# Group norm and attention on one core: constant products ahead of the input, a matrix product for the first group sums, eight open chains

## The chip, the cores and the metric

The kernel runs on one core of one Trainium2 chip. The metric is the device time of one execution in microseconds; a run's figure is that of its slowest core, and here there is only one core. The time before is the median of three runs.

## What is computed

The input x has 4 images of 512 channels and 48 x 48 pixels (2304 tokens). Each image goes through a group norm with 32 groups of 16 channels, a projection to q, k and v, attention with 8 heads of 64 channels, an output projection, and a residual sum. Cut to what matters:

```python
hn  = group_norm(x, gn_scale, gn_bias)              # 32 groups, eps 1e-5
qkv = einsum('oc,bchw->bohw', qkv_w, hn) + qkv_b    # float32
q, k, v = qkv.reshape(b, 3, 8, 64, t).astype(float16)
w = softmax(einsum('bhct,bhcs->bhts', q * s, k * s))
a = einsum('bhts,bhcs->bhct', w, v).astype(float32)
return x + einsum('oc,bchw->bohw', proj_w, a) + proj_b
```

A group's mean and variance need 16 channels, which are 16 partitions of the tile that holds x, so the sums have to cross partitions.

## The kernel before

Channels lie on partitions: an image is four chunks of 128 channels (index c), each in five token blocks (index j), four of 512 tokens and one of 256. Heads are treated in pairs, since two heads of 64 channels fill 128 partitions.

After an opening, a long stream runs over 16 groups (an image and a pair of heads), token blocks and bursts of key tiles. Each burst has scores on TensorE (L959), exponentials on ScalarE (L966), sums on VectorE (L1015) and the product with v on TensorE (L984). The projections of later groups (L709 for q and k, L760 for v, L848 for the output) are cut into pieces and put between the bursts. The order of every engine's instructions is the order in which the program issues them; each engine works in that order and waits on semaphores.

The change lies in the opening, which is what runs before the first scores. There the first image is loaded and normalised, and q and k of its first pair and v of its first two pairs are computed. What is needed to follow it:

- The loads. SP's queue brings the blocks of x chunk by chunk; two blocks of the first chunk and the first pair's weights go over ScalarE's queue; the four small vectors (scale, bias and so on) over GpSimd's. The remaining weights follow the last chunk of x on SP's queue.
- The small constants. GpSimd fills `mhalf`, `ones`, `ones16`, `fine`, `moments` and `nothing` (L571 to L923) after issuing its four loads.
- The statistics of a chunk. `stats` (L608) runs one VectorE pass over each block and `aggregate` (L612) joins the five into a mean and a variance per channel, in the columns of `moments`.
- From channels to groups. `group_scale` transposes `moments` on VectorE (L622), aggregates each half of 16 channels (L627), adds the epsilon (L629), raises to the power of minus one half on GpSimd (L631), and spreads the means back over the channels (L634). `coefficients` spreads the scales (L641), transposes back (L645) and forms a factor and an offset per channel (L651 to L653).
- The normalisation. `norm_chunk` applies them on ScalarE, block by block (L667), in place.
- The first chains. A chain is the sum over the four chunks for one block of q or k; `qk_steps` issues two products for a chunk, one for each half of 64 output columns (L709), and hands back the evacuation (L719, VectorE). Six chains stay open: the five blocks of k and the first of q. They take the six PSUM banks of the pool `ps_s`. When a chunk is normalised, its products go to all six. After the last chunk the six are evacuated, two at a time, and the other four blocks of q follow as closed chains (`qk_chain`), then the nine steps of v (`v_chain`).

VectorE's order in the opening is fixed by one loop: the statistics of the next chunk are placed between the coefficients of this one, with one block ahead of them for the first two chunks and two for the third.

PSUM has eight banks here: six in `ps_s`, one in `ps_av` (the products with v and the sums), one in `ps_w` (the projections in the stream and small products).

Of the kernel before, what the change touches and what calls it, by code (L numbers as in the profile page):

```python
# [12 lines left out]
F32 = mybir.dt.float32  # L13
F32R = mybir.dt.float32r
F16 = mybir.dt.float16
I32 = mybir.dt.int32
AF = mybir.ActivationFunctionType
ALU = mybir.AluOpType
# [6 lines left out]
GROUP = C // 32  # L25
EPS = 1e-5
P = 128
# [15 lines left out]
QB = 512  # L43
QBLOCKS = [(o, min(QB, T - o)) for o in range(0, T, QB)]
NQ = len(QBLOCKS)
# [422 lines left out]
def fast_path(  # L468
# [12 lines left out]
    nc = tc.nc  # L481

    RES = NC
    const = ctx.enter_context(tc.tile_pool(name="const", bufs=1))
# [4 lines left out]
    ppool = ctx.enter_context(tc.tile_pool(name="ppool", bufs=3))  # L489
# [3 lines left out]
    ps_s = ctx.enter_context(tc.tile_pool(name="ps_s", bufs=3, space=PSUM))  # L493
    ps_av = ctx.enter_context(tc.tile_pool(name="ps_av", bufs=1, space=PSUM))
# [24 lines left out]
    gsc = const.tile([P, NC], F32, name="gsc")  # L519
    gbi = const.tile([P, NC], F32, name="gbi")  # L520
# [49 lines left out]
    mhalf = const.tile([P, 2], F32, name="mhalf")  # L570
# [3 lines left out]
    ones16 = const.tile([P, D], F16, name="ones16")  # L574
    nc.gpsimd.memset(ones16, 1.0)

    fine = const.tile([P, 2 * QB // P], F32, name="fine")
    nc.gpsimd.memset(fine, 1.0)

# [4 lines left out]
    def chain_bank(name):  # L584
        if alone[0]:
            return ps_s.tile([P, 2, QB], F32, tag="ps", name=name)[:, 0, :]
        return ps_w.tile([P, QB], F32, tag="pw", name=name)

    def small_bank(name):
        return ps_w.tile([P, QB], F32, tag="pw", name=name)  # L590


    stat, coef, ab = {}, {}, {}
# [7 lines left out]
    moments = const.tile([P, 3, SQ], F32, name="moments")  # L601
    nc.gpsimd.memset(moments, 1.0)

    def stats(b, j, c):

        if b not in stat:
            stat[b] = small.tile([P, NC, NQ, 6], F32, tag="st", bufs=1, name=f"st_{b}")
        nc.vector.bn_stats(stat[b][:, c, j, :], hn[b, c, j])  # L608

    def aggregate(b, chunks=ALL):  # L610
        for c in chunks:
            nc.vector.bn_aggr(  # L612
                moments[:, 1:, c], stat[b][:, c].rearrange("p j s -> p (j s)")
            )

    def small_tile(n, tag):
        return small.tile([P, n], F32, tag=tag, bufs=1, name=tag)

    def group_scale(b, chunks=ALL):

        turned = small_tile(SQ * 3, "turned")
        nc.vector.transpose(  # L622
            turned.rearrange("p (c s) -> p s c", s=3), moments
        )
        grouped = small_tile(NGROUP * 2, "grouped").rearrange("p (g s) -> p g s", s=2)
        for i in range(NGROUP):
            nc.vector.bn_aggr(grouped[:, i, :], turned[:, bass.ts(i, GROUP * 3)])  # L627
        veps = small_tile(NGROUP, "veps")
        nc.vector.tensor_scalar(veps, grouped[:, :, 1], EPS, None, ALU.add)  # L629
        rstd = small_tile(NGROUP, "rstd")  # L630
        nc.gpsimd.tensor_tensor(rstd, veps, mhalf, ALU.pow)  # L631
        both = small_tile(SQ * 2, "both").rearrange("p (s c) -> p s c", s=2)
        spread = both.rearrange("p s (g j) -> p s g j", g=NGROUP)
        nc.vector.tensor_copy(  # L634
            spread[:, 0], grouped[:, :, 0:1].to_broadcast((P, NGROUP, GROUP))
        )
        coef[b, chunks[0]] = both, spread, rstd

    def coefficients(b, chunks=ALL):
        both, spread, rstd = coef.pop((b, chunks[0]))  # L640
        nc.vector.tensor_copy(  # L641
            spread[:, 1], rstd.unsqueeze(2).to_broadcast((P, NGROUP, GROUP))
        )
        cols = small_tile(SQ * 2, "cols").rearrange("p (s c) -> p s c", s=2)
        nc.vector.transpose(cols, both)  # L645
        cs = slice(chunks[0], chunks[-1] + 1)
        ga, mga, gb = (
            small.tile([P, NC], F32, tag=f"{n}{chunks[0] % 2}", name=f"{n}_{b}")[:, cs]
            for n in ("ga", "mga", "gb")
        )  # L650
        nc.vector.tensor_tensor(ga, cols[:, 1, cs], gsc[:, cs], ALU.mult)  # L651
        nc.vector.tensor_tensor(mga, cols[:, 0, cs], ga, ALU.mult)
        nc.vector.tensor_tensor(gb, gbi[:, cs], mga, ALU.subtract)  # L653
        for i, c in enumerate(chunks):
            ab[b, c] = ga[:, i : i + 1], gb[:, i : i + 1]

    def norm(b, j, c):
        t = hn[b, c, j]
        ga, gb = ab[b, c]
        nc.vector.tensor_scalar(t, t, ga, gb, ALU.mult, ALU.add)  # L660

    def norm_chunk(b, c):

        ga, gb = ab[b, c]
        for j in range(NQ):
            t = hn[b, c, j]
            nc.scalar.activation(t, t, AF.Identity, bias=gb, scale=ga)  # L667
# [27 lines left out]
    def qk_steps(g, part, j, bank=None):  # L695
        b, pr = divmod(g, NPAIR)
        o, n = QBLOCKS[j]
        pw = {0: bank}

        def one(c):  # L700
            if g not in qk:
                qk[g] = [
                    qkp.tile([P, T], F16, tag=a, name=f"{a}_{g}") for a in ("q", "k")
                ]
            if c == 0 and bank is None:
                pw[0] = chain_bank(f"pqk_{g}_{part}_{j}")
            w0 = part * C + pr * P
            for lo in (0, D):
                nc.tensor.matmul(  # L709
                    pw[0][lo : lo + D, :n],  # L710
                    wqkv[:, c, w0 + lo : w0 + lo + D],
                    hn[b, c, j],
                    start=(c == 0),
                    stop=(c == NC - 1),
                )

            def evacuate():
                col = part * NPAIR + pr
                nc.vector.tensor_scalar(  # L719
                    qk[g][part][:, o : o + n],  # L720
                    pw[0][:, :n],
                    bqkv[:, col : col + 1],
                    SCALE,
                    ALU.add,
                    ALU.mult,
                )

            if bank is not None:
                return evacuate
            if c == NC - 1:  # L730
                evacuate()

        return one

    def qk_chain(g, part, j):
        n = QBLOCKS[j][1]
        steps = qk_steps(g, part, j)
        return chain_pieces(n / 600.0, steps, HALVES if n == QB else WHOLE)
# [198 lines left out]
    av, acc, pts, avx, sums, rowd, ibs = {}, {}, {}, {}, {}, {}, {}  # L937

    stream = []
    for g in range(NG):  # L940
        for j, (o, n) in enumerate(QBLOCKS):
            count = NT * n // QB // BURST
# [255 lines left out]
    for b in range(B):  # L1198
        g = b * NPAIR
# [69 lines left out]

    six = [(1, j) for j in range(NQ)] + [(0, 0)]
    banks = [
        ps_s.tile([P, 2, QB], F32, tag="ps", name=f"ps_{i}") for i in range(3)
    ]
    chains = [qk_steps(0, *a, banks[i // 2][:, i % 2, :]) for i, a in enumerate(six)]

    def all_stats(c):
        for j in range(NQ):
            stats(0, j, c)  # L1280
        aggregate(0, (c,))

    all_stats(0)
    group_scale(0, (0,))
    for c in range(NC):

        for j in range(NQ):
            if j == (1 if c < 2 else 2):
                coefficients(0, (c,))
                norm_chunk(0, c)  # L1290
            if c + 1 < NC:
                stats(0, j, c + 1)
        if c + 1 < NC:
            aggregate(0, (c + 1,))
            group_scale(0, (c + 1,))
        for i, chain in enumerate(chains):
            evacuate = chain(c)
            if c == NC - 1 and i % 2 == 1:

                before()  # L1300
                evacuate()
            before = evacuate
    for j in range(1, NQ):
        for p in qk_chain(0, 0, j):
            p[1]()
    for i in range(0, NT, 2):
# [64 lines left out]
    for n in range(end):  # L1371
# [29 lines left out]
        if n - BEHIND in soon:  # L1401
            g, j = stream[n - BEHIND][:2]
# [9 lines left out]
    g, b, j = NG - 1, B - 1, NQ - 1  # L1412
    n = QBLOCKS[j][1]
# [6 lines left out]
    def last_banks(name):  # L1420
        return ps_s.tile([P, 2, QB], F32, tag="ps", name=name)
# [15 lines left out]
    def beyond(k, name, tag):  # L1437
        bank = chain_bank(name)
        _, store = last_run(k, bank)
        t = xpool.tile([P, QB], F32, tag=tag, name=f"beyond_{name}")  # L1440
        xt = res[b, k[0], k[1][0]].rearrange("p m n -> p (m n)")

        def copy():
            nc.scalar.copy(t, bank)

        def finish():
            nc.gpsimd.tensor_tensor(xt, t, xt, ALU.add)
            return store

        return copy, finish  # L1450
# [8 lines left out]
    copy, finish = beyond(ahead[0], "ahead_0", "x0_3")  # L1459
# [4 lines left out]
    for i, k in enumerate(todo[:NC]):  # L1464
        if i % 2 == 0:
            banks = last_banks(f"rest_{i}")
# [89 lines left out]
```

## Time and profile before

| | us |
|---|---|
| median of 3 runs | 1604.98 |
| lowest, highest | 1604.17, 1605.35 |
| profiled execution, its own time | 1605.03 |
| its span, first to last instruction | 1603.3 |
| TensorE busy (matmul) | 1577.8 (98%) |
| ScalarE busy | 1268.0 (79%) |
| VectorE busy | 1138.1 (71%) |
| GpSimd busy | 325.6 (20%) |

The opening by stretches, in the same profiled execution (us from the span's start; busy time of TensorE, VectorE, ScalarE and GpSimd):

| stretch | PE | DVE | ACT | POOL |
|---|---|---|---|---|
| 0 to 11.92, before the first product | 0 | 6.66 | 2.15 | 3.67 |
| 11.92 to 22.92, chunks 0 and 1 | 11.00 | 10.25 | 6.44 | 1.38 |
| 22.92 to 33.03, chunks 2 and 3 | 9.71 | 5.85 | 6.36 | 0.69 |
| 33.03 to 45.06, four more blocks of q | 12.03 | 3.65 | 0 | 0 |
| 45.06 to 76.24, v | 31.18 | 6.02 | 0 | 0 |

How to read it: the profile is one execution. PE is TensorE's matmul, PEld its weight load, DVE is VectorE, ACT ScalarE, POOL GpSimd, SP the engine that issues most loads and stores. In a line of the timeline the first number is the start, the second the time taken, then come the engine, the line of the kernel, the operation, what it writes and reads, and in brackets the idle time before it and what ended that. In a line of waits the three numbers are the total, the count and the longest. A float32 product appears as two matmuls and two weight loads.

### The profile page before, as it was taken

How to read it: one execution, taken by the hardware profiler on the slowest of the kernel's cores; microseconds unless marked ns; L12 is line 12 of the kernel's file. 1: busy time of each engine (PE TensorE's matmuls, PEld its weight loads, DVE VectorE, ACT ScalarE, POOL GpSimd, SP SyncE). 2: the span in 40 equal slices, each digit the busy share in tenths (PEclk: the TensorE clock that was granted, in tenths of full speed). 3: DMA queues.
4: the chain of work that ended last, by engine and by line, in shares of the span. 5: the costliest groups of instructions: out<-in, count | busy, mean ns of one | idle time of the engine just before them, and what ended most of it. 6: DMA issues, size and time to landing. Idle time of an engine off the chain costs nothing.

```text
span 1603.3 us, 28319 instructions
## 1 busy us (share of the span) xinstructions
PE 1577.8 (98%) x11500; PEld 692.1 (43%) x11500; DVE 1138.1 (71%) x1301; ACT 1268.0 (79%) x1362; POOL 325.6 (20%) x457
## 2 busy tenths in 40 slices
PE   6999999999999999999999999999999999999997
PEld 2533434443333534545333354455533334435544
DVE  6267668876666668887676666898766766667775
ACT  3077777888888888888888888887878888888895
POOL 1001202221121222322112121221212121122222
PEclk9999999999999999999999999999999999999998
DMA  7002021000000024521000001352100000015424
GB/s 216 9 14 64 14 59 29 18 15 11 14 15 12 15 64 120 147 67 28 11 14 18 14 12 41 112 156 87 25 15 18 15 15 11 15 31 177 137 67 128
DMA packets 94896, 82.10 MB, mean 51 GB/s; under 512 B 50852, under 2 KB 60964, under 8 KB 94756
## 3 DMA queue, kind: packets, MB, share of 16 engines
q1 hardware_dynamic: 92724, 78.35, 18.1%
q8 instruction: 92, 1.51, 0.4%
q10 hardware_dynamic: 1904, 1.84, 0.4%
q14 instruction: 48, 0.39, 0.1%
q0 software_dynamic: 128, 0.01, 0.0%
HBM read 60.70 MB, written 19.17 MB: 50 GB/s over the span
## 4 chain that ended last, share of the span: by engine, by line
PE 94%; DVE 3%; ACT 1%; DMA 1%; issue 0%; POOL 0%; SPq 0%; DVEq 0%
PE pqk L709 29%; PE ps L959 19%; PE av L984 19%; PE pv L760 15%; PE pr L848 8%; PE sl L1043 2%; ACT p L966 1%; PE ps L709 1%; DVE acc L1015 1%; DVE st L608 1%; DMA row<-inv 0%; DMA r<-x_dram 0%; DMA x<-x_dram 0%; DVE r L875 0%; DVE grouped L627 0%
## 5 line engine op out<-in xcount | busy, mean ns | idle before, releaser
L966 ACT ACTIVATE p<-ps 128x1024 f16<-128x1024 f32 x1296 | 1233.3, 1025 | 304.7 <-PE ps L959 301.8
L1015 DVE TENSOR_TENSOR acc<-acc,p 128x3072 f16<-128x3072 f16 x270 | 488.6, 1810 | 54.0 <-ACT p L966 51.6
L709 PE MATMUL pqk<-x,wqkv 128*64 128x512 f32 (+1 forms) x2464 | 517.1, 549 | 0.1
L984 PE MATMUL av<-p,v 128*64 128x512 f16 (+1 forms) x2880 | 360.8, 364 | 0.4 <-DVE slx L1059 0.3
L959 PE MATMUL ps<-q,k 64*128 64x512 f16 (+1 forms) x2880 | 356.1, 358 | 1.5 <-ACT p L966 1.1
L760 PE MATMUL pv<-wqkv,x 128*64 128x256 f32 x2304 | 267.5, 379 | 0.0
L709 PEld LDWEIGHTS pqk<-x,wqkv 128*64 128x64 f32 x2464 | 170.2, 137 | 210.7 <-issue 161.0
L1081 POOL TENSOR_SCALAR in<-sums 128x8 f32<-128x8 f32 (+1 forms) x158 | 102.7, 650 | 726.6 <-DMA sums<-slx 720.0
L959 PEld LDWEIGHTS <-k 64*128 64x128 f16 x2880 | 106.0, 94 | 288.5 <-issue 239.6
L984 PEld LDWEIGHTS <-v 128*64 128x64 f16 x2880 | 131.3, 109 | 213.2 <-issue 168.6
L1108 POOL TENSOR_TENSOR att<-avx,ib 128x512 f16<-128x512 f32 (+1 forms) x78 | 123.8, 1588 | 428.3 <-DMA ib<-row 378.4
L760 PEld LDWEIGHTS pv<-wqkv,x 128*64 128x64 f32 x2304 | 161.7, 137 | 85.4
L1015 DVE TENSOR_TENSOR acc<-p,p 128x3072 f16<-128x3072 f16 x79 | 138.1, 1748 | 0.0
L848 PE MATMUL pr<-a,whi 128*128 128x512 f32 (+1 forms) x311 | 121.9, 399 | 1.2 <-DVE r L875 0.6
L1020 DVE TENSOR_TENSOR acc<-acc 128x1024 f16<-128x1024 f16 x156 | 113.4, 727 | 3.3
L848 PE MATMUL pr<-a,wlo 128*128 128x512 f32 (+1 forms) x311 | 113.6, 373 | 0.0
L719 DVE TENSOR_SCALAR q<-pqk,bqkv 128x512 f16<-128x512 f32 (+1 forms) x79 | 54.9, 695 | 80.1 <-PE pqk L709 79.7
L768 DVE TENSOR_TENSOR v<-pv,bv 128x512 f16<-128x512 f32 x72 | 49.7, 690 | 82.4 <-PE pv L760 82.3
L719 DVE TENSOR_SCALAR k<-pqk,bqkv 128x512 f16<-128x512 f32 (+1 forms) x75 | 52.1, 695 | 77.4 <-PE pqk L709 77.2
L1059 DVE COPY slx<-sl 128x512 f32<-128x512 f32 (+1 forms) x79 | 50.6, 640 | 66.0 <-PE sl L1043 65.9
L875 DVE SCALAR_TENSOR_TENSOR r<-pr,bproj,r 128x512 f32<-128x512 f32 (+1 forms) x80 | 54.9, 694 | 43.1 <-PE pr L848 39.7
L993 DVE COPY avx<-av 128x512 f32<-128x512 f32 (+1 forms) x79 | 50.6, 640 | 37.6 <-PE av L984 37.2
(79 smaller groups left out, 474.3 us busy)
## 6 DMA issues: line engine op xcount, KB each, us to landing
r<-x_dram SPq DMA_DIRECT2D x72, 256.0 KB, 3.8
out_dram<-r SPq DMA_DIRECT2D x69, 256.0 KB, 2.6
ib<-row SPq DMA_DIRECT2D x126, 128.0 KB, 3.1
x<-x_dram SPq DMA_DIRECT2D x62, 256.0 KB, 4.1
x<-x_dram SPq DMA_DIRECT2D x16, 128.0 KB, 5.0
sums<-slx SPq DMA_DIRECT2D x128, 2.0 KB, 2.1
ib<-row SPq DMA_DIRECT2D x30, 64.0 KB, 3.1
wqkv<-qkv_wT_dram SPq DMA_DIRECT2D x2, 768.0 KB, 6.9
```

The source lines that it names most:

```text
L709: nc.tensor.matmul(pw[0][lo : lo + D, :n], wqkv[:, c, w0 + lo : w0 + lo + D], hn[b, c, j], start=(c == 0), stop=(c == NC - 1),)
L719: nc.vector.tensor_scalar(qk[g][part][:, o : o + n], pw[0][:, :n], bqkv[:, col : col + 1], SCALE, ALU.add, ALU.mult,)
L760: nc.tensor.matmul(pw[0][lo : lo + D, a, :], hn[b, c, i * P // QB][:, at + lo : at + lo + D], wqkv[:, c, 2 * C + half * C // 2 :][:, : C / ...
L848: nc.tensor.matmul(ps[:, :n], w[:, c, bass.ts(m, P)], at32[b, j, c], start=(i == 0), stop=(i == len(steps) - 1),)
L875: nc.vector.scalar_tensor_tensor(xt[:, i], places[i], bias, xt[:, i], ALU.add, ALU.add)
L959: nc.tensor.matmul(ps[:, h, a * n : (a + 1) * n], kt[rows, bass.ts(i, P)], qt[rows, o : o + n], start=True, stop=True,)
L966: nc.scalar.activation(pt[:, r], ps, AF.Exp)
L984: nc.tensor.matmul(av[0][lo : lo + D, :n], vv[b, pr // 2][:, i, pr % 2 * P + lo : pr % 2 * P + lo + D], pt[:, r, h, a * n : (a + 1) * n], ...
L1015: nc.vector.tensor_tensor(t, before, pt, ALU.add)
L1020: nc.vector.tensor_tensor(t[:, 0], t[:, 0], t[:, r], ALU.add)
L1081: nc.gpsimd.tensor_scalar(t, sm, limit, None, op)
L1108: nc.gpsimd.tensor_tensor(atts[g][:, o : o + n], avx.pop((g, j))[:, :n], ibs.pop((g, j))[:, :n], ALU.mult,)
```

## The change

It does four things, all in the opening.

1. VectorE fills a tile with ones, and TensorE multiplies it by itself 16 times ahead of the first chunk's statistics and four times after its group products. The results are not read. The tile is a buffer of the exponentials' pool; the results go to the bank of `ps_av`.
2. A matrix `share` of 128 x 128 is made on GpSimd, with 1/16 where row and column lie in the same group and zero elsewhere.
3. For the first chunk alone, `first_group` takes the place of `group_scale` and `coefficients`: the means of the groups are a product of `share` with the column of means, the variances a second product with the variance plus squared deviation, and the factor and offset follow without a transpose. The other three chunks keep the old way.
4. Eight chains stay open: the five blocks of k and the first three of q. The two new ones use the banks of `ps_av` and `ps_w`. Two blocks of q are left for closed chains.

```diff
+    share = const.tile([P, P // GROUP, GROUP], F32, name="share")
+    nc.gpsimd.memset(share, 1.0 / GROUP)
+    for sign, base in ((1, 0), (-1, GROUP - 1)):
+        nc.gpsimd.affine_select(
+            out=share, in_=share, compare_op=ALU.is_ge, fill=0.0, base=base,
+            pattern=[[-sign * GROUP, P // GROUP], [0, GROUP]],
+            channel_multiplier=sign,
+        )
...
+    def first_group():
+        mean, var = moments[:, 1, 0:1], moments[:, 2, 0:1]
+        by = share.rearrange("p g j -> p (g j)")
+        pm = small_bank("first_group")
...
+        nc.tensor.matmul(pm[:, 0:1], by, mean, start=True, stop=True)
+        nc.vector.tensor_tensor(dev, mean, pm[:, 0:1], ALU.subtract)
+        nc.vector.tensor_scalar(var2, dev, dev, var, ALU.mult, ALU.add)
+        nc.tensor.matmul(pm[:, 1:2], by, var2, start=True, stop=True)
+        nc.vector.scalar_tensor_tensor(
+            mg, pm[:, 0:1], -1.0, gsc[:, 0:1], ALU.mult, ALU.mult
+        )
+        nc.vector.tensor_scalar(veps, pm[:, 1:2], EPS, None, ALU.add)
+        nc.gpsimd.tensor_tensor(rstd, veps, mhalf[:, 0:1], ALU.pow)
+
+        def finish():
+            ga, gb = small_tile(1, "first_ga"), small_tile(1, "first_gb")
+            nc.vector.tensor_tensor(ga, rstd, gsc[:, 0:1], ALU.mult)
+            nc.vector.tensor_scalar(gb, rstd, mg, gbi[:, 0:1], ALU.mult, ALU.add)
+            ab[0, 0] = ga, gb
+        return finish
...
-    six = [(1, j) for j in range(NQ)] + [(0, 0)]
-    banks = [
-        ps_s.tile([P, 2, QB], F32, tag="ps", name=f"ps_{i}") for i in range(3)
-    ]
-    chains = [qk_steps(0, *a, banks[i // 2][:, i % 2, :]) for i, a in enumerate(six)]
+    busy = ppool.tile([P, 2, QB], F16, tag="p", name="busy")
+    nc.vector.memset(busy[:, 0, :], 1.0)
+    idle = ps_av.tile([P, QB], F32, tag="av", name="idle")
+
+    def keep_busy(count):
+        for _ in range(count):
+            nc.tensor.matmul(
+                idle, busy[:, 0, :P], busy[:, 0, :], start=True, stop=True
+            )
...
+    keep_busy(16)
     all_stats(0)
-    group_scale(0, (0,))
+    first_coefficients = first_group()
+    keep_busy(4)
+
+    eight = [(1, j) for j in range(NQ)] + [(0, j) for j in range(8 - NQ)]
...
+    banks.append(ps_av.tile([P, QB], F32, tag="av", name="first_av"))
+    banks.append(small_bank("first_w"))
+    chains = [qk_steps(0, *a, bank) for a, bank in zip(eight, banks)]
...
-                coefficients(0, (c,))
+                if c == 0:
+                    first_coefficients()
+                else:
+                    coefficients(0, (c,))
...
-    for j in range(1, NQ):
+    for j in range(8 - NQ, NQ):
         for p in qk_chain(0, 0, j):
             p[1]()
```

The added lines move the later ones: L709 becomes L748, L719 becomes L758, and L760 becomes L799 in the kernel after. The new group sums stand at L678 to L691, the constant products at L1317, and the matrix at L578 and L580. On GpSimd the fills of `fine` and `moments` come after the matrix, and the pool configuration that stood just before the power now stands before the two selections.

More of the change, by code (lines that the diff above doesn't have):

```diff
@@ L575, in fast_path @@
     nc.gpsimd.memset(ones16, 1.0)
+    share = const.tile([P, P // GROUP, GROUP], F32, name="share")
+    nc.gpsimd.memset(share, 1.0 / GROUP)
+    for sign, base in ((1, 0), (-1, GROUP - 1)):
+        nc.gpsimd.affine_select(
+            out=share,
+            in_=share,
+            compare_op=ALU.is_ge,
+            fill=0.0,
+            base=base,
+            pattern=[[-sign * GROUP, P // GROUP], [0, GROUP]],
+            channel_multiplier=sign,
+        )
     fine = const.tile([P, 2 * QB // P], F32, name="fine")
@@ L655, in coefficients @@
             ab[b, c] = ga[:, i : i + 1], gb[:, i : i + 1]
+    def first_group():
+        mean, var = moments[:, 1, 0:1], moments[:, 2, 0:1]
+        by = share.rearrange("p g j -> p (g j)")
+        pm = small_bank("first_group")
+        dev, var2, mg, veps, rstd = (
+            small_tile(1, f"first_{n}") for n in ("dev", "var2", "mg", "veps", "rstd")
+        )
[14 more added lines that the diff above has]
+        return finish
     def norm(b, j, c):
@@ L1268, in fast_path @@
         put_qk(g + 5, 0)
-    six = [(1, j) for j in range(NQ)] + [(0, 0)]
-    banks = [
-        ps_s.tile([P, 2, QB], F32, tag="ps", name=f"ps_{i}") for i in range(3)
-    ]
-    chains = [qk_steps(0, *a, banks[i // 2][:, i % 2, :]) for i, a in enumerate(six)]
+    busy = ppool.tile([P, 2, QB], F16, tag="p", name="busy")
[5 more added lines that the diff above has]
+                idle, busy[:, 0, :P], busy[:, 0, :], start=True, stop=True
+            )
     def all_stats(c):
@@ L1281, in all_stats @@
         aggregate(0, (c,))
+    keep_busy(16)
     all_stats(0)
-    group_scale(0, (0,))
+    first_coefficients = first_group()
+    keep_busy(4)
+    eight = [(1, j) for j in range(NQ)] + [(0, j) for j in range(8 - NQ)]
+    banks = [
+        t[:, i, :]
+        for k in range(3)
+        for t in (ps_s.tile([P, 2, QB], F32, tag="ps", name=f"ps_{k}"),)
+        for i in range(2)
+    ]
+    banks.append(ps_av.tile([P, QB], F32, tag="av", name="first_av"))
+    banks.append(small_bank("first_w"))
+    chains = [qk_steps(0, *a, bank) for a, bank in zip(eight, banks)]
     for c in range(NC):
```

## The prediction, made before the changed kernel ran

> **What bounds the kernel now.** I read the page first, then the waits of TensorE, then the opening 45 us as a timeline and as stretches. The page's chain of waits and its slices:
>
> ```profile
> PE 94%; DVE 3%; ACT 1%; DMA 1%; issue 0%; POOL 0%; SPq 0%; DVEq 0%
> ...
> PE   6999999999999999999999999999999999999997
> ```
>
> TensorE carries the end; only the first and last slices have room. The waits of TensorE's matmul queue over the whole run say where:
>
> ```profile
> PE ps L709 <- DMA x<-x_dram: 11.9, 1, 11.9
> PE count L1495 <- DVE good L1494: 2.1, 1, 2.1
> PE ps L959 <- ACT p L966: 1.1, 3, 0.5
> ```
>
> Half of what is ever idle lies before the first product, at 11.92 us. The change works there and nowhere else, so what is to be found is when TensorE finishes the opening projections: the first product of v (L760) starts at 45.06. The timeline of the opening:
>
> ```profile
> 7.59 0.29 DVE L612 BATCH_NORM_AGGREGATE moments<-st 128x2 f32<-128x30 f32 x1
> ...
> 9.22 0.72 POOL L631 TENSOR_TENSOR rstd<-veps,mhalf 128x2 f32<-128x2 f32 x1 [5.14 <-DVE both L634]
> ...
> 10.86 0.16 DVE L653 TENSOR_TENSOR gb<-gbi,mga 128x1 f32<-128x1 f32 x1
> ...
> 11.05 3.42 ACT L667 ACTIVATE x<-x,gb,ga 128x512 f32<-128x512 f32 x5 [5.04 <-DVE gb L653]
> ...
> 13.69 0.24 PEld L709 LDWEIGHTS ps<-x,wqkv 128*64 128x64 f32 x2 [0.62 <-issue]
> ...
> 15.03 0.14 PEld L709 LDWEIGHTS ps<-x,wqkv 128*64 128x64 f32 x2 [0.29 <-issue]
> 15.46 0.14 PEld L709 LDWEIGHTS ps<-x,wqkv 128*64 128x64 f32 x2 [0.29 <-issue]
> ...
> 23.31 9.89 PE L709 MATMUL ps<-x,wqkv 128*64 128x512 f32 x48 [0.39 <-ACT x L667]
> ```
>
> The reader sees the chain to the first chunk (statistics end 7.88, offsets 11.02, normalised block, product 11.92); weight loads 0.86 us apart up to 14.54 and 0.43 apart from 15.03, so the first products run at half rate; and a wait of 0.39 at 23.31, because six chains finish chunk 1 before chunk 2 is normalised.
>
> Stated as a sum: at full rate a 512-column chain takes 8 steps of 0.429 us (loads from 33.04 to 39.90 are 16 such steps), 3.43 us, and a 256-column chain 1.715. Ten chains, 8 x 3.43 + 2 x 1.715, are 30.87 us. They take 45.06 - 11.92 = 33.14 now, so 2.27 us are lost: 1.57 in the first two chunks (11.00 for 9.43 of work, the half rate) and the rest, 0.7, in the waits for chunks 2 and 3.
>
> [...] these stretches (duration, PE busy, PEld, DVE, ACT, POOL, clock, DMA)
>
> ```profile
> 1591.61:1595.02 3.41, 1.71 (x11) 1.07 (x9) 3.11 (x7) 0.41 (x1) 3.16 (x5) 1.00 0.58 214
> 1595.02:1596.00 0.98, 0.19 (x2) 0.09 (x2) 0.98 (x3) 0.00 (x0) 0.00 (x0) 0.50 1.03 372
> ```
>
> have the clock halved after a stretch of a window's length that was half busy, 1.6 us after the last dense product. [...] the pool configuration now stands before the power of L631, at 4.1 us, and the power starts at 9.22, within 0.16 us of its input, so up to 5.1 us could be hidden.
>
> **The change part by part.** All against the profiled run's own time, 1605.03 us (span 1603.3 plus 1.7 around it), 0.05 above the median shown.
>
> *Products on constants.* A DVE fill of 128x512 f16 (under 0.5 us, done before the first block lands at 4.68), then 16 products of 512 columns. SP issues its first DMA at 0.80, so TensorE is free by then and they start near 1.4. At full rate a 512-column pass is about 0.215 us (an estimate: half of a 0.429 step, which is two passes), at half 0.43. With 2.7 to 3.4 us at half rate they end near 6.3; wholly at half rate, 16 x 0.43 = 6.9, at 8.3. TensorE has nothing else until 7.9, so they cost 0 to 0.4 us, taken as 0. Four more (0.9 us) come after the group products, near 9.3 to 10.2, before x is there. If the clock survives, 1.57 us of half rate go.
>
> *Group sums by a product.* Removed from chunk 0: transpose, two aggregates, two spreads, a transpose back, one multiply, 7.91 to 11.02. Added: two float32 products of one column with 128x128 weights. The nearest row is the one-column product at the end (its input ready 1595.40, its reader started 1595.91, so at most 0.5 us round trip); the larger weight loads are 0.19 each (L848), two per product. From both sides, 0.35 to 0.6; taken 0.45. The chain is then: 7.88, product to 8.37, deviation and variance at the 0.2 pitch of L651 to L653 to 8.77, product to 9.27. L682 reads the tile of that product too and stands ahead of L685, so 0.08 + 0.17 more, 9.52; the power 9.6 to 10.3 (0.7 as in L631); factor and offset 0.2 each, 10.7. That is 0.3 earlier than 11.02, with 0.0 to 0.8 as ends. Behind the two waits on DVE stand chunk 1's statistics. Its first block moves from 9.05 to 9.6 and its other four follow the offsets, as now, so chunk 1 is not later. The product waits for the 16 on TensorE's queue, counted above.
>
> *The matrix on POOL.* Fill, pool configuration and two selections of 128x128 go ahead of the fill of moments (now 3.86), which L625 needs at 7.59. Selections have no row; 128x256 float32 steps at L1479 take 0.85, so 0.4 to 0.85 each[...]. 3.82 + 0.2 + 0.1 + 2 x 0.7 + 0.25 is 5.8: hidden, with 1.8 to spare. A configuration that stalls is rival C.
>
> *Eight chains.* A chunk then holds 7 x 0.857 + 0.43 = 6.43 us of products in place of 4.72, against 5.5, 5.9 and 4.9 us between chunks' readiness (11.73, 17.3, 23.1, 28.1). No chunk is then waited for: starting at 11.6, chunk 0 ends at 18.0, chunk 1 (ready 17.1) at 24.5, chunk 2 (ready 23) at 30.9. The 0.7 us of waits go. Two chains rather than four follow. The extra evacuations are the same L719 rows in another place; the two borrowed banks are next needed by the stream, after 76 us, and cost nothing. The constant tile's buffer is free long before the first exponentials. No DMA moves on SP, and the weights of v are there by 24 us, bv by 40, ahead of the first v evacuation near 44. What is late next is nothing but TensorE itself.
>
> The sum: 11.92 - 0.3 + 30.87 = 42.5 in place of 45.06, 2.55 earlier. What follows is TensorE's dense stream to the end and shifts as one. 1605.0 - 2.5 = 1602.5.
>
> **The rivals.** A, the sum above: the clock survives the pause. For it: [...] the longest pure pause is about 1.6 us (to 7.9, and 10.2 to 11.6). Against it: the tail row above. 0.50.
>
> B, the clock falls in the pause. From about 6.3 to 11.6 only 0.9 us of constants and two tiny products run, less than half of any window inside it, and half busy did not hold the clock in the tail. Chunk 0 then runs 1.7 to 3.4 us at half rate, 1.4 us lost as now, but no longer beside a wait. 1605.0 - 2.5 + 1.4 = 1603.9. 0.26.
>
> C, slower: POOL's configuration stalls before the first selection. [...] It costs nothing up to 1.8 us of stall, and turns the change into a loss when the stall exceeds about 3 us (B's gain of 1.1 plus the slack of 1.8). For it: the configuration now stands on the path. Against: the power that follows it now is an ordinary operation and ran at once. 0.12.
>
> D, more: the group products and the one-column power take their low ends and the offsets come 0.8 to 1.1 us earlier, everything else as in A: 1605.0 - 3.3 = 1601.7. Against it: one-element steps of this chain have a pitch of 0.2 us, and nine stages remain. 0.12.
>
> **How the numbers follow.** The forecast is A, 1602.5. A itself spans 1601.9 to 1603.2 by the bounds of the product and the power; B reaches to 1605.0 by its window's phase. 1601.4 to 1605.3 takes in A, B and most of D and leaves out C. About 0.2% (3.2 us) is what a measurement of this kernel tells from no change; most cases lie within. Faster by more: half of D and the upper tail of A, 0.14. Slower by more: the worse part of C, 0.06. Within: 0.80.
>
> **What would show it.** Right: the first L748 product at 11.4 to 11.8, weight loads 0.43 apart from the first, no wait before chunk 2, first v product near 42.5. Clock: loads 0.86 apart after 11.6 is B. POOL: moments filled after 7.4 is C. The prediction is wrong if the first v product shifts by 2.5 us and the span does not follow, which would mean that something outside the opening binds the stream.

## The result, and the profile after

The changed kernel takes 1601.62 us (median of 19 executions, 1600.59 to 1604.47) against 1604.42 for the kernel before on the same chips, a ratio of 0.9984 with a 95% interval of 0.9978 to 0.9990: some 2.8 us less, where 2.5 were forecast. A second series (below) gives 0.9988, 0.9979 to 0.9996. The profiled execution has a span of 1601.2 and took 1602.89 in all; it is one of the longer ones, for a reason shown at the end of this section.

The page's slices and its chain of waits. Compared with before, the first digit of TensorE is 9 in place of 6:

```profile
PE   9999999999999999999999999999999999999997
...
PE 96%; DVE 1%; ACT 1%; DMA 1%; POOL 0%; issue 0%; SPq 0%; DVEq 0%
```

The opening in the timeline of the changed kernel (start, time taken, engine, line, what):

```profile
1.52 6.47 PE L1317 MATMUL idle<-busy 128*128 128x512 f16 x16 [1.52 <-DVE busy L1312]
...
4.16 0.75 POOL L580 TENSOR_SCALAR_AFFINE_SELECT share<-share 128x128 f32<-128x128 f32 x2
...
4.90 0.18 POOL L615 MEMSET moments<- 128x96 f32 x1
...
7.78 0.29 DVE L625 BATCH_NORM_AGGREGATE moments<-st 128x2 f32<-128x30 f32 x1
...
9.07 0.38 PE L681 MATMUL first_group<-first_var,share 128*128 128x1 f32 x2 [0.56 <-DVE first_var L680]
...
9.31 1.02 PE L1317 MATMUL idle<-busy 128*128 128x512 f16 x4
...
10.49 0.27 DVE L691 TENSOR_SCALAR first_gb<-first_rstd,first_mg,gbi 128x1 f32<-128x1 f32 x1
...
11.67 4.94 PE L748 MATMUL ps<-x,wqkv 128*64 128x512 f32 x24 [1.34 <-ACT x L706]
...
18.16 4.89 PE L748 MATMUL ps<-x,wqkv 128*64 128x512 f32 x24
...
42.64 2.54 PE L799 MATMUL pv<-wqkv,x 128*64 128x256 f32 x22
```

The reader sees the matrix and `moments` ready at 5.1, long before the aggregate at 7.78; the first projection product at 11.67; chunk 1's first product at 18.16 with no idle time in front of it; and the first v product at 42.64 in place of 45.06. The first block of x landed 0.19 us later than in the profile before (statistics from 4.87, not 4.68), so 2.42 us is slightly less than the change is worth.

Did the clock hold through the pause? Two stretches of 3.41 us, the length of a clock window as the changes in the runs below show it (duration, PE busy, PEld, DVE, ACT, POOL, clock, DMA share, GB/s), from the rise at 7.30:

```profile
7.30:10.71 3.41, 2.34 (x11) 0.93 (x9) 2.21 (x11) 0.00 (x0) 0.58 (x1) 1.00 1.11 330
10.71:14.13 3.42, 2.46 (x12) 0.91 (x14) 3.32 (x9) 3.33 (x5) 0.00 (x0) 1.00 1.05 371
```

With 2.34 and 2.46 us of work out of 3.41, both run at the full clock: the constants cover enough here. The clock column reads 1.00 before a first rise as well (in the kernel before for 11.92 to 14.65, where the loads are 0.86 us apart); the rise itself shows in the weight loads of the constants, which are 0.43 us apart up to 7.04 and 0.35 at the next.

After the opening the shift was to stay. I set each of the 2880 score products (L959, now L998) against the same one of the kernel before. The difference is -2.42 us at 76 us and -2.68 at 1025; at 1052 it drops to -0.94, in one jump; at the last score product it is -1.25. Not all of this is the change's: three of the runs below whose openings are no more than 0.6 us from that of before (without constants, constants alone, group product alone) also move by -0.25 to -0.31 up to 1025 us, by some -0.5 near 1052, where TensorE waits in the profile before, and by some -0.3 at the end, so there the one profile before had lost time. The waits of the changed kernel from 1030 to 1056 us show the jump:

```profile
DVE r L914 <- DMA r<-x_dram: 3.3, 1, 3.3
...
PE pr L887 <- DVE r L914: 2.2, 1, 2.2
```

A residual block, 6.9 us from its issue at 1041.97 to its landing, is late by 3.3 us and holds up VectorE's evacuation, and TensorE behind it by 2.2. In the profile before the same place costs 1.1 and 0.4. SP issues eight loads of x and a spread of sums just before it, which may be what holds it up; that was not tried apart. The second profile of the same kernel, at the end of the experiments, shows how far the place varies.

### The profile page after: what moved, and what is told of

It reads as the page before. It is cut to its first block, busy times and chain, and to the rows that moved or that the text cites. A ratio compares the mean times of both kernels' runs of the same rounds, so it can differ in the third digit from the quotient of the medians.

```text
span 1601.2 us, 28364 instructions
## 1 busy us (share of the span) xinstructions
PE 1583.9 (99%) x11524; PEld 695.0 (43%) x11524; DVE 1137.0 (71%) x1298; ACT 1268.1 (79%) x1362; POOL 327.9 (20%) x460
## 4 chain that ended last, share of the span: by engine, by line
PE 96%; DVE 1%; ACT 1%; DMA 1%; POOL 0%; issue 0%; SPq 0%; DVEq 0%
PE pqk L748 29%; PE ps L998 20%; PE av L1023 20%; PE pv L799 15%; PE pr L887 8%; PE sl L1082 2%; PE ps L748 1%; ACT p L1005 1%; DMA x<-x_dram 0%; DMA r<-x_dram 0%; DVE acc L1054 0%; PE first_av L748 0%; PE first_w L748 0%; DVE st L621 0%; POOL a L879 0%
## 5 line engine op out<-in xcount | busy, mean ns | idle before, releaser
L1005 ACT ACTIVATE p<-ps 128x1024 f16<-128x1024 f32 x1296 | 1233.3, 1025 | 302.5 <-PE ps L998 299.5
L748 PE MATMUL pqk<-x,wqkv 128*64 128x512 f32 (+1 forms) x2432 | 510.2, 549 | 0.1
L998 PE MATMUL ps<-q,k 64*128 64x512 f16 (+1 forms) x2880 | 356.2, 358 | 1.5 <-ACT p L1005 1.1
L799 PE MATMUL pv<-wqkv,x 128*64 128x256 f32 x2304 | 267.5, 379 | 0.0
L748 PEld LDWEIGHTS pqk<-x,wqkv 128*64 128x64 f32 x2432 | 168.0, 137 | 205.9 <-issue 156.2
L998 PEld LDWEIGHTS <-k 64*128 64x128 f16 x2880 | 106.0, 94 | 288.5 <-issue 239.6
L799 PEld LDWEIGHTS pv<-wqkv,x 128*64 128x64 f32 x2304 | 161.7, 137 | 85.4
L758 DVE TENSOR_SCALAR k<-pqk,bqkv 128x512 f16<-128x512 f32 (+1 forms) x75 | 52.1, 695 | 77.4 <-PE pqk L748 77.2
L758 DVE TENSOR_SCALAR q<-pqk,bqkv 128x512 f16<-128x512 f32 (+1 forms) x77 | 53.4, 694 | 74.6 <-PE pqk L748 74.4
```

Source lines behind the costliest of these rows:

```text
L748: nc.tensor.matmul(pw[0][lo : lo + D, :n], wqkv[:, c, w0 + lo : w0 + lo + D], hn[b, c, j], start=(c == 0), stop=(c == NC - 1),)
L758: nc.vector.tensor_scalar(qk[g][part][:, o : o + n], pw[0][:, :n], bqkv[:, col : col + 1], SCALE, ALU.add, ALU.mult,)
L799: nc.tensor.matmul(pw[0][lo : lo + D, a, :], hn[b, c, i * P // QB][:, at + lo : at + lo + D], wqkv[:, c, 2 * C + half * C // 2 :][:, : C / ...
L998: nc.tensor.matmul(ps[:, h, a * n : (a + 1) * n], kt[rows, bass.ts(i, P)], qt[rows, o : o + n], start=True, stop=True,)
L1005: nc.scalar.activation(pt[:, r], ps, AF.Exp)
```

## The experiments

The change has three parts that can be put in alone: the constants (C), the group product (S) and the eight chains (E). Together with the kernels before and after, six runs fill in all eight combinations.

### The changed kernel without the constants (S and E)

```diff
-    keep_busy(16)
     all_stats(0)
     first_coefficients = first_group()
-    keep_busy(4)
```

> The changed kernel without any of the 20 constant products; group product and eight chains stay. My theory (the constants buy the full clock, and with eight chains nothing hides the half rate any more): the first projection product still starts at 11.5 to 11.8, its weight loads 0.86 us apart for 1.7 to 3.5 us, and the first v product comes at 43.8 to 44.5 in place of 42.64; the time is 1.2 to 1.7 above the changed kernel, so 1.0 to 1.6 below the kernel before. Rival (the constants are worth nothing, since the wait for x hid the half rate in the kernel before): first v product at 42.6, time as the changed kernel.

1604.51 us, ratio to before 0.9999 (0.9991 to 1.0007). The whole gain is gone. First projection product at 12.00, first v product at 45.27. Weight loads of that opening:

```profile
15.47 0.24 PEld L748 LDWEIGHTS ps<-x,wqkv 128*64 128x64 f32 x2 [0.61 <-issue]
16.32 0.24 PEld L748 LDWEIGHTS ps<-x,wqkv 128*64 128x64 f32 x2 [0.62 <-issue]
16.93 0.14 PEld L748 LDWEIGHTS ps<-x,wqkv 128*64 128x64 f32 x2 [0.37 <-issue]
17.36 0.14 PEld L748 LDWEIGHTS ps<-x,wqkv 128*64 128x64 f32 x2 [0.29 <-issue]
```

The distance halves at 16.7, so the half rate lasted 4.67 us, longer than the 3.5 that I had allowed. Half of it, 2.3 us, is the loss. The rest of the miss is the later start.

### The kernel before with eight chains alone (E)

> The kernel before with eight open chains in place of six, and nothing else of the change. My theory: the waits for chunks 2 and 3 (0.7 us) go, the half rate stays, now unhidden: first projection product at 11.92, first v product at 44.3 to 44.6 in place of 45.06, time 0.4 to 0.8 below the kernel before. Rival (the chains are the whole gain): first v product before 43.2, time 2 or more below.

The edit is the list `eight`, its banks and the shorter closing loop, as in the change. 1604.39 us, ratio 0.9999 (0.9991 to 1.0008); first v product at 45.22. The rival falls. My theory missed the place as well: the waits are gone, but the half rate, which no longer lies beside them, was 4.65 us long in this profile and 2.73 in the profile before. With 2.73 the sum that is used below would put the first v product at 44.2. The 0.4 to 0.8 us that the theory gave lie inside the interval, so it is not shown that the chains alone bring nothing, only that it is too little to tell here. The weight loads show the end of the half rate:

```profile
16.27 0.24 PEld L709 LDWEIGHTS ps<-x,wqkv 128*64 128x64 f32 x2 [0.62 <-issue]
16.87 0.14 PEld L709 LDWEIGHTS ps<-x,wqkv 128*64 128x64 f32 x2 [0.36 <-issue]
```

### The kernel before with constants alone (C)

```diff
+    keep_busy(16)
     all_stats(0)
+    keep_busy(12)
     group_scale(0, (0,))
```

> The kernel before with sixteen and then twelve constant products ahead of the first projection, six chains and the old sums. My theory (six chains then wait for x): full rate from the first product at 11.92, chunk 0 done at 16.6 and chunk 1 waited for until 17.3, chunks 2 and 3 waited for as before; first v product at 45.0 to 45.1, time within 0.3 of the kernel before. Rival (the constants are worth their 1.6 us by themselves): first v product at 43.5, time 1.5 below.

1603.92 us, ratio 0.9996 (0.9988 to 1.0004); first v product at 45.01. As expected: full rate from the first product, and the time turns into waits for x ahead of chunk 1 and chunk 2.

```profile
11.87 4.94 PE L709 MATMUL ps<-x,wqkv 128*64 128x512 f32 x24 [1.68 <-ACT x L667]
17.42 4.94 PE L709 MATMUL ps<-x,wqkv 128*64 128x512 f32 x24 [0.61 <-ACT x L667]
23.26 9.89 PE L709 MATMUL ps<-x,wqkv 128*64 128x512 f32 x48 [0.90 <-ACT x L667]
```

### The kernel before with the group product alone (S)

> The kernel before with the first chunk's group sums by the matrix product, and nothing else. With TensorE cold the two products take 0.59 each in place of 0.38, so the offsets come hardly earlier: first projection product at 11.6 to 12.0, first v product within 0.3 of 45.06, time within 0.4 of the kernel before.

1604.01 us, ratio 0.9995 (0.9987 to 1.0004). First projection product at 11.86, as expected; first v product at 45.64, 0.58 later than before and out of my bound, since the clock rose only at 17.55 in this execution, 5.7 us after the first product. On a cold TensorE the product is worth next to nothing:

```profile
7.56 0.29 DVE L625 BATCH_NORM_AGGREGATE moments<-st 128x2 f32<-128x30 f32 x1
8.53 0.16 DVE L679 TENSOR_TENSOR first_dev<-moments,first_group 128x1 f32<-128x1 f32 x1 [0.68 <-PE first_group L678]
...
10.68 0.27 DVE L691 TENSOR_SCALAR first_gb<-first_rstd,first_mg,gbi 128x1 f32<-128x1 f32 x1
```

Each product makes VectorE wait 0.68 us, against 0.47 warm. From the end of the aggregate to the end of the offset it is 3.10 us (10.95 less 7.85), against 3.14 by the transposes and 2.69 in the changed kernel (10.76 less 8.07).

### The changed kernel with six chains (C and S)

> The changed kernel with six open chains in place of eight; the constants and the group product stay. My theory (six chains give TensorE 4.72 us of work a chunk, less than the 5 to 6 us between chunks, so the full clock only turns into waits): first projection product at 11.67, waits of 0.5 to 1 ahead of chunks 1 and 2, first v product at 44.7 to 44.9 in place of 45.06, time 0.2 to 0.6 below the kernel before. Rival (the chains are a small part of the gain, since alone they showed none): first v product at 43.3 or earlier, time 1.8 or more below.

The edit takes back the list `six` and its loop. 1603.85 us, ratio 0.9993 (0.9985 to 1.0001); first v product at 44.57. That is a little more than I expected, 1.1 us by the ratio, and its interval reaches no change; the earlier offsets are most of what is left. In this execution the clock was taken away at 11.05 and given back at 14.46, and it cost next to nothing, since a wait for chunk 2 is left (0.21).

### The changed kernel with the old sums (C and E)

```diff
-    first_coefficients = first_group()
-    keep_busy(4)
+    group_scale(0, (0,))
+    keep_busy(12)
...
-                if c == 0:
-                    first_coefficients()
-                else:
-                    coefficients(0, (c,))
+                coefficients(0, (c,))
```

> The changed kernel with the first chunk's group sums by the transposes of the other chunks; sixteen constant products, then twelve more at once, to about 10.6, so that the clock is held. My theory (the matrix product is worth 0.2 to 0.3): first projection product at 11.9 to 12.1 in place of 11.67, first v product at 42.9 to 43.1, time 0.3 above the changed kernel. Rival (it is worth most of the gain): first v product after 43.6, time 1 or more above.

1602.13 us, ratio 0.9987 (0.9980 to 0.9994); first projection product at 11.99, first v product at 42.96, 0.3 after the changed kernel, as expected. The 20 executions fall into two heaps: eleven from 1600.82 to 1602.16, each with a mean clock of 0.998, and nine from 1603.06 to 1604.27, each with 0.997. By an estimate from the 3.41 us between changes of the clock, one window at half the clock is 0.5 x 3.41 / 1600 = 0.001 of the mean and 1.7 us of time, which is about the distance between the heaps. Of 138 executions of the kernel before, in three series, two have 0.997 and the others more. So with the old sums the constants, which all come early here, seem to fail to hold the clock in nearly half of the executions; the one profile, of the faster heap, kept it.

All eight together (first v product in the profile; ratio of times to the kernel before):

| constants | group product | chains | first projection product | first v product | ratio |
|---|---|---|---|---|---|
| no | no | 6 | 11.92 | 45.06 | 1 |
| yes | no | 6 | 11.87 | 45.01 | 0.9996 |
| no | yes | 6 | 11.86 | 45.64 | 0.9995 |
| no | no | 8 | 11.95 | 45.22 | 0.9999 |
| no | yes | 8 | 12.00 | 45.27 | 0.9999 |
| yes | yes | 6 | 11.49 | 44.57 | 0.9993 |
| yes | no | 8 | 11.99 | 42.96 | 0.9987 |
| yes | yes | 8 | 11.67 | 42.64 | 0.9984 |

Only where constants and eight chains stand together does the opening shrink by 2 us, and only there does the interval of the ratio exclude 1. Each needs the other.

### Sixteen constants and none after the group products

```diff
     first_coefficients = first_group()
-    keep_busy(4)
```

> The changed kernel without the four constant products after the group products; the sixteen stay. If a window less than half busy takes the clock away: chunk 0 runs at half rate in most executions, first v product near 43.9, time 0.8 to 1.5 above the changed kernel. If only a window that is wholly idle does: full rate throughout, first v product at 42.6, time as the changed kernel.

1603.84 us, ratio 0.9996 (0.9987 to 1.0004), some 2 us above the changed kernel in ratio (0.9996 less 0.9984 of 1604). First projection product at 11.67, first v product at 44.34. It is the first case that came, and a little more than it said. Stretches of a window's length, cut at the clock's own changes:

```profile
5.22:8.63 3.41, 2.12 (x10) 0.89 (x8) 2.83 (x7) 0.98 (x1) 0.00 (x0) 1.00 1.14 306
8.63:12.05 3.42, 0.76 (x4) 0.49 (x6) 2.81 (x10) 1.24 (x2) 0.58 (x1) 1.00 1.06 378
12.05:15.46 3.41, 3.41 (x10) 0.92 (x8) 3.10 (x11) 2.18 (x4) 0.70 (x1) 0.50 1.04 377
```

The window with 2.12 us of work kept the clock, the one with 0.76 lost it at its end, at 12.05, and after the next, with 3.41, it was back, at 15.46. That the windows are 3.41 us long can be read from the changes themselves: they are 6.83 and 3.41 us apart here, 6.83 and 3.41 in the six-chain run, 6.82 and 6.83 in the run with the late matrix. Each of the 13 executions has a mean clock of 0.997 or less, so the loss is not this profile's alone. The six-chain run gives a closer miss: 1.65 us of 3.41, and the clock is lost.

```profile
7.64:11.05 3.41, 1.65 (x8) 0.83 (x8) 2.32 (x9) 0.43 (x1) 0.58 (x1) 1.00 1.09 350
11.05:14.46 3.41, 2.97 (x8) 1.01 (x10) 3.27 (x11) 3.00 (x5) 0.17 (x1) 0.50 1.05 381
```

The closest that held is in the run with constants alone, 1.73 us of 3.41:

```profile
9.93:13.34 3.41, 1.73 (x10) 0.55 (x10) 3.24 (x10) 2.34 (x4) 0.00 (x0) 1.00 1.05 381
13.34:16.76 3.42, 3.42 (x20) 1.08 (x16) 2.99 (x13) 1.29 (x3) 0.69 (x1) 1.00 1.06 382
```

With the tail of the kernel before (1.71 us, lost), these openings and tails show the clock lost at 1.71 us of work and less and kept at 1.73 and more, but for one tail that lost it at 1.73 (the run with the group product alone). It is no rule for all work, as the run with the general path shows below.

### Sixteen and eight

```diff
-    keep_busy(4)
+    keep_busy(8)
```

> Eight constant products after the group products in place of four, which fill the pause up to about 11.1. If the slow tail of the changed kernel (up to 1604.5) comes from executions in which the clock falls in the pause: the tail goes, median 0.2 to 0.6 below the changed kernel, first v product at 42.6. If the tail comes from elsewhere in the stream: nothing changes, median within 0.3.

1601.51 us, ratio 0.9980 (0.9973 to 0.9988); first v product at 42.55; 16 executions from 1600.62 to 1602.85. The median is no different from the changed kernel's; the upper end is 1.6 lower. Of the changed kernel's 19 executions two have a mean clock of 0.997, at 1603.22 and 1604.47, which fits a lost window. The others above 1602.6 have 0.998, and the profiled one among them is long by the late residual. So the tail seems to have both causes; with so few executions their shares are not settled. In the second series of the changed kernel five of 13 executions have 0.997, from 1602.54 to 1604.08.

### Sixteen and eight, and an earlier offset

```diff
         nc.vector.scalar_tensor_tensor(
-            mg, pm[:, 0:1], -1.0, gsc[:, 0:1], ALU.mult, ALU.mult
+            mg, dev, mean, gsc[:, 0:1], ALU.subtract, ALU.mult
         )
```

> As the run with sixteen and eight constant products, and the product of mean and scale is formed from deviation and mean, so that it no longer reads the tile that the second group product writes and does not wait for it. It takes some 0.08 off the chain to the offsets: first projection product near 11.6, first v product near 42.55, time 0.0 to 0.2 below that run, which these rounds can hardly tell.

1601.51 us, ratio 0.9982 (0.9975 to 0.9989), 18 executions from 1600.88 to 1603.27; first projection product at 11.34, first v product at 42.31, where the first block had landed 0.17 earlier than in the run with sixteen and eight. No gain that these executions can tell. Three of them have a mean clock of 0.997 or less, so eight products in the pause may not hold the clock in all. No version tried is clearly better than the changed kernel.

### The matrix made late

```diff
-    for sign, base in ((1, 0), (-1, GROUP - 1)):
+    for sign, base in ((1, 0), (-1, GROUP - 1)) * 7:
```

> The changed kernel with fourteen selections on GpSimd in place of two (the twelve more repeat the same two and leave the matrix as it is), at 0.37 each by the changed kernel's trace, 4.5 us in all. The fill of moments then ends near 9.6 in place of 5.1. My theory (slack of 2.7 us before the aggregate at 7.78, and no slack from there on): aggregate at 9.6, first projection product at 13.5, first v product at 44.4 or, with the clock down after the longer pause, up to 46; time 1.7 to 3.3 above the changed kernel. If what follows had slack of its own: less than 1 above.

1606.84 us, ratio 1.0017 (1.0010 to 1.0024), slower than both: about 5.3 us above the changed kernel by the two ratios, more than expected. The timeline:

```profile
4.16 5.63 POOL L580 TENSOR_SCALAR_AFFINE_SELECT share<-share 128x128 f32<-128x128 f32 x14
...
9.78 0.18 POOL L615 MEMSET moments<- 128x96 f32 x1
```

and VectorE's wait for it:

```profile
9.99 0.29 DVE L625 BATCH_NORM_AGGREGATE moments<-st 128x2 f32<-128x30 f32 x1 [2.55 <-POOL nothing L962]
```

The aggregate is 2.2 us late, not 1.8 (14 selections at 0.40 rather than 0.37), the first projection product 2.41 late, at 14.08. Behind it comes what I had undersized: the clock, lost at 11.07 after a window with 0.38 us of work, returned only at 17.90, so that 3.8 us ran at half rate, 1.9 of loss, and the first v product came at 46.93, 4.3 late. The last 1.0 of the 5.3 is no part of that profile, whose execution was the shortest of the series at 1605.93. This is the price of the rival that the prediction named as slower: there is 2.7 us of cover ahead of the aggregate and none after it.

One of its 21 executions took 3174 us and is not in the ratio. The kernel ends with a test of its own sums, which sets a flag; if it fails, a second, general version of the whole computation runs behind the first. To see whether the long execution had taken this general path, I turned the comparison of the flag round, so that every execution takes both paths:

```diff
-    nc.vector.tensor_scalar(flag, pf, P * every - 0.5, None, ALU.is_lt)
+    nc.vector.tensor_scalar(flag, pf, P * every - 0.5, None, ALU.is_ge)
```

> The changed kernel with the comparison that sets the flag turned round, so that the general path runs after the fast one in every execution. It gives the time of an execution that takes both. One of the 21 executions with the late matrix took 3174 us. If that execution took the general path after the fast one, this run takes 3170 to 3180; if something else held it up, this run takes clearly another time.

6093 us. The long execution did not take the general path; what held it up stays open.

The profile of this run tells something else. Up to the flag it is the changed kernel, so its opening is a further one of that kernel, and there the clock was lost in the pause:

```profile
7.73:11.14 3.41, 1.65 (x8) 0.83 (x8) 2.33 (x9) 0.69 (x1) 0.59 (x1) 1.00 1.08 356
11.14:14.55 3.41, 3.23 (x8) 1.00 (x10) 3.27 (x10) 2.73 (x5) 0.42 (x1) 0.50 1.06 381
```

The clock had risen at 4.32, the sixteen ended at 6.51 in place of 7.99, and the window with the pause held only 1.65 us of work. The first v product came at 43.88, 1.24 later than in the first profile, although the first projection product, at 11.32, was 0.35 earlier. This is the prediction's rival B. And in the general path the clock also falls at the end of windows that the records show full:

```profile
5588.52:5591.93 3.41, 3.41 (x15) 0.99 (x13) 2.95 (x6) 2.00 (x3) 0.00 (x0) 1.00 0.00 0
5591.93:5595.34 3.41, 2.67 (x7) 0.60 (x7) 2.91 (x7) 0.00 (x0) 0.00 (x0) 0.50 0.00 0
```

Of the 101 falls in this execution 38 follow windows of 2.5 us of work or more. So busy matmul time alone does not decide everywhere; what else does is open.

### The changed kernel once more

> The changed kernel once more, for a second profile and more executions. If the late load of a residual near 1045 us in its first profile belongs to that execution alone: no jump there this time, every later score product some 2.4 to 2.8 us earlier than in the kernel before up to the end, and a median of 1601.2 to 1602.0. If the shift of the opening provokes it: a jump of more than 1 us at the same place.

1602.75 us against 1605.07 for the kernel before in the same series, ratio 0.9988 (0.9979 to 0.9996). The median is higher than I said, but so is that of before. First projection product at 11.60, first v product at 42.57. The score products are 2.49 us earlier at 76 us, 2.81 at 1025 and 2.51 at the end; the jump at the late residual is 0.61 in place of 1.75, with the residual 2.1 us late. In the run with sixteen and eight, whose opening is as short, it is 0.33. The 0.61 lies between my two cases. With the opening as short in all three, the cost of the place changes from one execution to the next. Other profiles do not settle whether an earlier opening makes it likelier: TensorE waits 0.4 us there in the run with the earlier offset (score products 2.8 us earlier than before), not at all with the old sums (2.1 earlier), and 0.3 with the late matrix (1.9 later).

## Why the prediction was right

The time, 1601.62, lies within the range and 0.9 below the figure; the forecast gain of 2.5 stands against 2.8 by the medians, 2.42 in the opening of the first profile and 2.49 in that of the second. As a bare number 1601.62 lies nearer to rival D's 1601.7 than to A, but the kernel before also came out 0.6 lower on these chips than the 1605.0 that the forecast started from, and the offsets were ready 0.26 us earlier (10.76 for 11.02), not the 0.8 to 1.1 that D needs. So it is A, in the executions that keep the clock. By its own steps:

- *The sum.* Its form was right: start of the first product, plus 30.87 us of work, plus half of the time at half rate. Four eight-chain profiles give it back. After: 11.67 + 30.87 = 42.54, measured 42.64. Without constants: 12.00 + 30.87 + 4.67 / 2 = 45.21, measured 45.27. Chains alone: 11.95 + 30.87 + 4.65 / 2 = 45.15, measured 45.22. Late matrix: 14.08 + 30.87 + 3.82 / 2 = 46.86, measured 46.93.
- *The split of the loss* was the weak term. I had put 1.57 us to the half rate and 0.7 to waits, as if each part of the change could take its own. Taken alone each gives nothing that can be told from no change (0.9996 and 0.9999), since with six chains a faster start only waits longer for x, and with eight chains a slow start has no wait to hide beside. Nor is the half rate 1.57: half of the 2.73 us in the profile before is 1.37, and in two others it lasted 4.65 and 4.67 us and cost 2.3. Only the sum of the two parts was right.
- *The constants.* The sixteen ended at 7.99, not near 6.3, since the clock rose late, at 7.30, 5.78 us after the first of them, where I had estimated 2.7 to 3.4 (2.73 in the profile before); still before the aggregate's end at 8.07, so they cost 0 as taken. The four after the group products are worth 2 us: without them most of the gain is gone.
- *The clock in the pause.* A was the likeliest and is what two profiles of the changed kernel show; but what I gave against it, the half-busy stretch of the tail (1.71 us of 3.41), is what the runs bear out in this pause: windows with 0.76 and with 1.65 us of work out of 3.41 lost the clock. That the clock outlives a pure pause of 1.6 us, which is what stood for A, no trace had shown. A held in the first profile because the sixteen ended 1.7 us later than I had reckoned and so filled the window with 2.34. That was luck: the clock rose at 7.30, 6.35 and 4.32 in three profiles of this opening, and only the first two rises came late enough. My count of 0.9 us of work in the pause was for an earlier end; where they did end early, at 6.51 in the run that takes both paths, B came. Seven of the 32 timed executions of the changed kernel have a mean clock of 0.997, which fits B, so A is what most of them do, not all.
- *The group product.* Taken at 0.3 us (0 to 0.8); measured 0.45 from aggregate to offset, and 0.04 when TensorE is cold. The sum used 0.49 and 0.50 for the two products where it had settled on 0.45; from the aggregate's end to the reader's start it was 0.48 (8.07 to 8.55). That this step leans on the constants too was not seen. The later landing of x ate 0.19 of it in the profile.
- *The matrix on POOL.* Selections of 0.37 in place of 0.7, `moments` full at 5.1 in place of 5.8, no stall behind the pool configuration: 4.16 is where the first selection starts, at once after the fill (3.86 to 4.08). So C falls; a stall in that place was an assumption, which no trace had shown. What a matrix that comes late costs, the run with the late matrix shows: 5.3 us for an aggregate 2.2 us late.
- *Eight chains.* No wait ahead of chunks 1 to 3, as predicted; the two borrowed banks cost nothing that the trace shows.
- *The stream shifts as one.* Nearly: it moved by another 0.26 up to 1025 us, as it does in runs with the old opening, and lost 1.75 at one late residual in the first profile, 0.61 in the second.

## What to carry to other kernels

Two losses that lie beside each other were worth nothing one at a time here (ratios 0.9996 and 0.9999): an engine that starts slow while its input is late must get both more work and its full clock, or the gain of one turns into the other's wait. Where a pause is to be bridged with idle products, put them inside the pause and look at every clock window that could cover it, not only at the longest gap: here the one over the pause lost the clock with 0.76 us of work out of 3.41 and kept it with 2.34. A change of 2 us in 1600 is read from the place where it acts (here the start of the first v product), since one late load elsewhere in the same execution is as large (1.75 us of shift lost at the residual here).

## What the hardware showed beyond what was expected

- In these openings and tails the clock was lost at the end of windows of 3.41 us that held 0.38 to 1.73 us of work (the last in the tail of the run with the group product alone) and kept after windows that held 1.73 to 2.46. As the fall came at the window's end, the pause showed its cost later: in the run with sixteen constants and none in the pause at 12.05, when the first projection product had started at 11.67. In the general path the clock also fell after windows busy for the whole 3.41 (at 5591.93, for one).
- The rise took more work in a window than the clock's keeping did: the six-chain run, busy from 1.52, had its clock raised at 4.22, after 2.70 us of work in that window; the run with the old sums, busy from 1.52 too, had a window end at 4.15 (3.41 before its rise at 7.56), with 2.64 us in it, and was not raised. The records do not draw the line closer: in the run with the late matrix the window from 11.07 held 2.71 us and did not raise it. The two eight-chain profiles without constants ran at half rate for over 4.6 us.
- A float32 product of one column with 128x128 weights took TensorE 0.38 us at full clock (the changed kernel) and 0.59 at half (the group product alone), and VectorE waited 0.47 and 0.68 for it.
- A selection of 128x128 float32 on GpSimd took 0.37 us in the changed kernel (0.75 for two) and 0.40 in the run with the late matrix (5.63 for fourteen).
